# Where the key tiles of the setup are kept, and where the router's small steps stand, in a decoder layer on one core

## The chip, the core and the metric

The kernel runs on one core of one Trainium2 chip. The metric is the device time of one execution in microseconds (us); the time of a kernel is the median of its runs. The engines are named as in the profile: PE is TensorE with its matrix products (PEld its weight loads), DVE is VectorE, ACT is ScalarE, POOL is GpSimd, and SP is the engine whose queue issues the DMA transfers. A product's result lies in PSUM, in one of eight banks that the program cycles through, and is copied from there to SBUF by DVE or ACT.

## The reference, cut to what matters

One decoder layer over x of 16 x 512 x 256 (float32), in three stages, each added to x and normalised:

```
x = LN(x + self_attention(x))        # linear attention, 16 heads, two key and value maps
x = LN(x + cross_attention(x, ctx))  # 16 heads of 64; context 16 x 64 x 256
x = LN(x + experts(x))               # 8 experts, 256 -> 1024 -> 256, chosen by a router

q = x @ Wq.T
k, v = split(context @ Wkv.T)        # keys and values of the context, 1024 wide each
sim = q @ k.T / 8;  out = softmax(sim) @ v @ Wout.T + b_out
routing_weights = softmax(x @ router_w.T + router_b)
```

The change touches the setup of cross attention (the keys k of all 16 batches, and v times Wout) and the setup of the router.

## The kernel before, in words

**Stages.** Before the first batch can run, a setup of some 80 to 190 us makes what all batches share. The context (1024 rows of 256) and Wkv (2048 x 256) are loaded and transposed on PE (line 233). Then `context_rows(r, q)` makes one tile of 128 features by 512 context rows: two products of 128 x 512 (line 436), copied from PSUM to an SBUF tile named `st`. For r = 0 to 7 these are keys: there are 8 x 2 = 16 such key tiles, and each is stored to DRAM (`k_dram`, line 464). For r = 8 to 15 they are values: each tile is multiplied with Wout (`ps_vo`, line 486), the products are copied to tiles named `vst`, and these are stored to DRAM (`vo_dram`, line 491).

**Tiles.** Both `st` and `vst` are tiles of the pool `sp`. The tag `st` has two places of 512 columns, the tag `vst` four places of 2 x 264 = 528. A new tile gets the place that was given out longest ago, and the instruction that writes it waits until all that read the old tile, its store included, are done.

**The copy out of PSUM.** `evac` (lines 182 to 188) gives copies to ACT and DVE in turn, so each added or moved `evac` also changes which engine gets the following ones.

**The router.** Its weight, 8 x 256, is loaded into a corner of the tile `early`. `router_columns` (line 371) centres it on DVE (lines 374 to 376), transposes it on PE (line 379) and copies the result to the last columns of `m` (line 380). `router_weights` (line 382) transposes Wq and Wo on PE (line 389), broadcasts three biases on DVE (lines 396 and 398), and multiplies Wo and the biases with the router's columns (line 403). Wq lies in `early`, Wo in `wo`; both, and wv, are loaded by `rest_of_weights` (line 354), in which DVE adds the identity to Wq and wv (line 319).

**Beside it.** In the same stretch, the Gram products of the first batches are made (`ps_g`, lines 549 and 554, from tiles `gx` of x, two places), their block is transposed (line 567), and every four batches `key_sums` follows (line 579). The first batch's self attention begins with line 623 (`ps_gk`) and 635 (`ps_s`). `output_weights` (line 509) loads Wout in two tiles `nato` and transposes them (line 522), and multiplies them with the router's columns (line 531). Then the values begin.

**What sets the order.** Six Python generators (Grams, context, self attention, cross attention, routing, experts) emit instructions piece by piece. A small model of the engines (`Model`) estimates when each instruction ends. `weave` always continues the generator that is furthest behind its plan among those that are ready. `yield` ends a piece; `yield WAIT` ends it and holds the generator back until the model says that its last piece is through; `until(...)` holds it back until a condition holds, `made(tile)` being that the tile is written by the model's clock. The order so found is then fixed for PE, DVE, ACT and POOL (`in_order`, line 1023), so each of them works strictly in that order. The DMA issues on SP are ordered by the compiler's own scheduler, and SP too works in order.

In `all_grams` the router's steps stand between the Grams:

```
if b == 1:
    router_columns(rw)      # one piece: DVE, then PE, then DVE
    yield
if b == QB - 1:
    cs.update(rest_of_weights(sp))
    yield from router_weights(sp)
```

## Time and profile before

| | |
|---|---|
| median of 3 runs | 1394.06 us (1392.28 to 1394.08) |
| the profiled execution's own time | 1391.12 us |
| its span in the profile | 1389.4 us |
| mean granted PE clock | 0.995 |
| PE busy, 0 to 10, 10 to 20, 20 to 30, 30 to 40 us | 6.44, 6.77, 7.87, 8.83 us of 10 |
| DMA share, the same stretches | 0.74, 0.97, 0.96, 0.63 |
| stores of key tiles | 16, 256 KB each, 3.5 us to landing in the median |
| stores of value products | 132 KB each, 2.4 us to landing in the median |

The busy time of PE includes products whose ends are modelled, so a busy PE may still run at a low clock: that is read from the granted clock, which is 1.00 at full speed. A row of the timeline gives the start, the duration, the engine, the line, the operation, the tile written and the tiles read, the count of records merged in the row, and in brackets how long the engine sat idle before it and what ended that. One float32 product appears as two records, so "x8" is four products. A row of the windows gives the stretch and its length, PE's busy time with the number of records, the granted clock, the DMA share and the GB/s moved.

### The profile page before, as it was taken

The page shows a single profiled execution, that of the slowest core. Times are in us where ns is not written, and L with a number is a line of the kernel's source. Part 1 is how long each engine was busy: PE and PEld are TensorE (multiplying, and loading weights), DVE is VectorE, ACT ScalarE, POOL GpSimd, SP SyncE. Part 2 cuts the span into 40 slices and gives each one's busy share as a digit, 9 for nine tenths or more (in the row PEclk, how much of TensorE's full clock was granted, in tenths as well). Part 3 has the DMA queues.
Part 4 walks back from the last instruction along what each step waited for, and adds up shares of the span by engine and source line. Part 5 has one row for each costly group of instructions (what it writes and reads, how often), then busy time and mean ns, then how long its engine had stood idle before and what let it go on. Part 6 is the DMA issues. An engine that isn't in the chain of part 4 may idle for free.

```text
span 1389.4 us, 24206 instructions
## 1 busy us (share of the span) xinstructions
PE 1363.8 (98%) x9630; PEld 1075.8 (77%) x9630; DVE 850.5 (61%) x1957; ACT 402.2 (29%) x912; POOL 203.9 (15%) x140
## 2 busy tenths in 40 slices
PE   7999999999999999999999999999999999999997
PEld 4666676877878787878878787878888787878686
DVE  2345848466583848476584848475675939484744
ACT  1134323132232314142233223142323323232322
POOL 0001112112020111112020112112020202111200
PEclk9999999999999999999999999999999999999999
DMA  8657775511516153421606053513334061505211
GB/s 261 202 121 193 201 188 169 141 32 33 154 46 157 46 141 106 123 80 47 186 18 169 31 141 106 126 62 75 112 94 124 16 187 46 147 26 126 91 55 40
DMA packets 98373, 153.57 MB, mean 111 GB/s; under 512 B 15561, under 2 KB 70097, under 8 KB 98257
## 3 DMA queue, kind: packets, MB, share of 16 engines
q1 hardware_dynamic: 98256, 151.98, 39.9%
q8 instruction: 78, 1.28, 0.4%
q14 instruction: 39, 0.31, 0.1%
HBM read 114.71 MB, written 37.22 MB: 109 GB/s over the span
## 4 chain that ended last, share of the span: by engine, by line
PE 90%; DVE 6%; DMA 2%; ACT 1%; issue 0%; SPq 0%; DVEq 0%; ACTq 0%
PE ps_x L828 17%; PE ps_sim L808 15%; PE ps_e L957 15%; PE ps_h L940 14%; PE ps_p L705 4%; PE ps_gk L623 4%; PE ps_o L681 3%; PE ps_kv L436 3%; PE ps_t L233 2%; PE ps_vo L486 2%; PE ps_kq L745 2%; PE ps_s L635 2%; PE ps_g L549 2%; PE ps_zt L694 1%; PE ps_m L664 1%; PE ps_g L554 1%
## 5 line engine op out<-in xcount | busy, mean ns | idle before, releaser
L940 PE MATMUL ps_h<-head_T,wi 128*128 128x256 f32 x1024 | 239.1, 379 | 0.0
L828 PE MATMUL ps_x<-vo,pT 32*128 32x264 f32 x4096 | 234.4, 385 | 3.7 <-DVE pT L798 3.7
L808 PE MATMUL ps_sim<-kq,x1T 128*128 128x512 f32 x512 | 235.0, 593 | 0.0
L828 PEld LDWEIGHTS ps_x<-vo,pT 32*128 32x128 f32 x4096 | 212.5, 186 | 24.5 <-issue 5.6
L940 PEld LDWEIGHTS ps_h<-head_T,wi 128*128 128x128 f32 x1024 | 193.4, 190 | 38.8 <-issue 13.0
L796 POOL TENSOR_TENSOR s<-s,sm 128x1024 f32<-128x1024 f32 x64 | 121.8, 1903 | 539.1 <-DVE sm L795 500.7
L835 DVE TENSOR_TENSOR x<-ps_x,x 128x264 f32<-128x264 f32 x64 | 23.2, 426 | 225.6 <-PE ps_x L828 225.6
L816 ACT ACTIVATE s<-s 128x512 f32<-128x512 f32 x128 | 80.7, 630 | 276.0 <-DVE s L815 276.0
L808 PEld LDWEIGHTS ps_sim<-kq,x1T 128*128 128x128 f32 x512 | 94.5, 190 | 83.2 <-issue 74.2
L814 DVE TENSOR_REDUCE mx<-ps_sim 128x8 f32<-128x512 f32 x128 | 86.1, 672 | 42.2 <-PE ps_sim L808 41.9
L815 DVE TENSOR_TENSOR s<-ps_sim,mx 128x512 f32<-128x512 f32 x128 | 88.5, 692 | 4.4
L719 POOL TENSOR_TENSOR x<-x,bout 128x1056 f32<-128x1056 f32 x16 | 38.8, 2422 | 320.9 <-ACT hT L946 172.6
L798 DVE STREAM_TRANSPOSE pT<-s 128x1024 f32<-128x1024 f32 x64 | 78.6, 1228 | 7.0 <-POOL s L796 7.0
L946 ACT ACTIVATE hT<-ps_h 128x256 f32<-128x256 f32 x128 | 47.0, 377 | 119.9 <-PE ps_h L940 119.7
L695 ACT ACTIVATE zT<-ps_zt,shift,gain 128x512 f32<-128x512 f32 x32 | 23.2, 776 | 189.7 <-PE ps_zt L694 189.7
L794 DVE TENSOR_REDUCE sm<-s 128x16 f32<-128x1024 f32 x64 | 77.1, 1204 | 0.4 <-ACT s L816 0.4
L267 ACT ACTIVATE x<-x,off,rstd 128x264 f32<-128x264 f32 (+1 forms) x112 | 58.3, 591 | 29.3 <-DVE off L265 29.3
L681 PE MATMUL ps_o<-m,xT 128*128 128x264 f32 x256 | 66.7, 387 | 0.0
L261 ACT ACTIVATE rstd<-bn_mv,eps 128x4 f32<-128x4 f32 (+1 forms) x70 | 20.7, 295 | 158.6 <-DVE bn_mv L250 155.1
L948 DVE TENSOR_SCALAR hT<-ps_h 128x256 f32<-128x256 f32 x128 | 52.1, 409 | 22.5 <-PE ps_h L940 22.3
L705 PE MATMUL ps_p<-wo,zT 128*128 128x264 f32 x256 | 63.1, 387 | 0.0
L436 PE MATMUL ps_kv<-cT,wT 128*128 128x512 f32 x128 | 61.1, 612 | 0.2 <-ACT vst L186 0.2
(172 smaller groups left out, 1892.6 us busy)
## 6 DMA issues: line engine op xcount, KB each, us to landing
vo<-vo_dram SPq DMA_DIRECT2D x512, 132.0 KB, 4.1
vo_dram<-vst SPq DMA_DIRECT2D x128, 132.0 KB, 2.4
xt<-in_x_dram SPq DMA_DIRECT2D x16, 512.0 KB, 4.0
wi<-L_ffn_experts_inter_dram SPq DMA_DIRECT2D x8, 1024.0 KB, 5.1
gx<-in_x_dram SPq DMA_DIRECT2D x15, 512.0 KB, 4.2
x_rest<-x SPq DMA_DIRECT2D x14, 512.0 KB, 3.0
out_dram<-x SPq DMA_DIRECT2D x14, 512.0 KB, 2.9
k_dram<-st SPq DMA_DIRECT2D x16, 256.0 KB, 3.5
```

Of the source, the lines that this page charges most:

```text
L436: nc.tensor.matmul(ps, wT[:, cc, r % 4 * P:(r % 4 + 1) * P], cT[:, cc, q * 512:(q + 1) * 512], start=(cc == 0), stop=(cc == NC - 1),)
L681: nc.tensor.matmul(ps[:, :CX], xT[:, cc, t * P:(t + 1) * P], m[:, cc, :], start=(cc == 0), stop=(cc == NC - 1))
L705: nc.tensor.matmul(ps[:, :CX], zT[:, cc, t * P:(t + 1) * P], wo[:, cc, :], start=(cc == 0), stop=(cc == NC - 1))
L796: nc.gpsimd.tensor_mul(s, s, sm.unsqueeze(2).to_broadcast([P, NH, J]))
L798: nc.vector.transpose(probsT[:, :, t, :], s.rearrange("p h (a j) -> p (h a) j", a=2))
L808: nc.tensor.matmul(ps, x1T[:, cc, t * P:(t + 1) * P], kq[:, cc, hf * 512:(hf + 1) * 512], start=(cc == 0), stop=(cc == NC - 1),)
L814: nc.vector.tensor_reduce(mx[:, hs], sim, AX.X, ALU.max)
L815: nc.vector.tensor_sub(s[:, hs, :], sim, mx[:, hs].unsqueeze(2).to_broadcast([P, 8, J]))
L816: nc.scalar.activation(s[:, hs, :], s[:, hs, :], AF.Exp, scale=SCALE)
L828: nc.tensor.matmul(ps[q][:, :CX], probsT[pq, blk].rearrange("p t i -> p (t i)"), vos[c][pq, i, :], start=(c == 0 and i == 0), stop=(c == 7 ...
L940: nc.tensor.matmul(ps[:, :TB], wi[:, cc, f * P:(f + 1) * P], head_T[b][:, cc, t0 * P:t0 * P + TB], start=(cc == 0), stop=(cc == NC - 1),)
L957: nc.tensor.matmul(ps[:, :C], hT[f][:, t * P:(t + 1) * P], wo_[:, f, :], start=(f == 0), stop=(f == NF - 1),)
```

## The change

Three edits, all in the setup.

1. Key tiles of rows 1, 2, 4, 5 and 7 take their place from the tag `vst` (four places) and use its first 512 columns; rows 0, 3 and 6, and all value tiles, stay with `st` (two places). The order of key tiles runs through six places in turn.
2. `router_columns` becomes a generator with a `yield WAIT` between its steps on DVE and its transposes on PE, and begins only when `early` is written by the model's clock.
3. After `rest_of_weights` the generator ends its piece, and `router_weights` begins only when `early` and `wo` are written by the model's clock.

```diff
 def router_columns(rw):
     nc.vector.tensor_reduce(rs, rw, AX.X, ALU.add)
     nc.vector.tensor_scalar(rs, rs, -1.0 / C, 1.0 / C, ALU.mult, ALU.add)
     nc.vector.tensor_scalar(rw, rw, rs[:, 0:1], None, ALU.add)
+    yield WAIT
     ps = bank("ps_rw")
...
 def context_rows(r, q):
...
-    st = sp.tile([P, 512], FP, tag="st", name="st")
+    if r % 3 and r < NP:
+
+        st = sp.tile([P, 2, CX], FP, tag="vst", name="stk", bufs=4)
+        st = st.rearrange("p a c -> p (a c)")[:, :512]
+    else:
+        st = sp.tile([P, 512], FP, tag="st", name="st")
     evac(st, ps)
...
 def all_grams():
...
         if b == 1:
-            router_columns(rw)
+            yield from until(lambda: made(early))
+            yield from router_columns(rw)
             yield
         if b == QB - 1:
             cs.update(rest_of_weights(sp))
+            yield
+            yield from until(lambda: made(early, wo))
             yield from router_weights(sp)
```

No product, copy or transfer is added or left out. The order in which the engines meet them is made anew by `weave`.

## The prediction

> **What bounds the kernel now.** I read the page first, then the timeline of the first 75 us, then the chain of waits, then the granted clock microsecond by microsecond. The page's engine row:

> ```profile
> PE 1363.8 (98%) x9630; PEld 1075.8 (77%) x9630; DVE 850.5 (61%) x1957; ACT 402.2 (29%) x912; POOL 203.9 (15%) x140
> ```

> TensorE (PE) is busy for 98% of a span of 1389.4 us and holds 90% of the chain that ends last. A change can save only where PE stands still or runs at a low clock. The change lies in the setup, so I looked for such places between 17 us (first key product) and 82 us. The timeline shows one large hole (start, duration, engine, line; in brackets the idle time before it and what ended it):

> ```profile
> 25.99 1.88 PE L436 MATMUL ps_kv<-cT,wT 128*128 128x512 f32 x4
> ...
> 27.12 0.69 DVE L188 COPY st<-ps_kv 128x512 f32<-128x512 f32 x1 [3.79 <-DMA k_dram<-st]
> ...
> 29.47 0.69 DVE L188 COPY st<-ps_kv 128x512 f32<-128x512 f32 x1 [1.65 <-DMA k_dram<-st]
> 30.07 0.40 DVE L374 TENSOR_REDUCE rs<-early 8x1 f32<-8x256 f32 x1
> ...
> 30.68 0.34 DVE L376 TENSOR_SCALAR early<-early,rs 8x256 f32<-8x256 f32 x1
> ...
> 31.17 0.35 PE L379 MATMUL ps_rw<-ident,early 8*128 8x8 f32 x2 [3.30 <-DVE early L376]
> ...
> 31.45 3.52 PE L549 MATMUL ps_g<-gx 128*128 128x257 f32 x8
> ...
> 40.12 1.90 PE L549 MATMUL ps_g<-gx 128*128 128x257 f32 x8
> ```

> Read it from the bottom up. PE waits 3.30 us for L376, a small VectorE (DVE) step of the router. L376 is not slow: L374 to L376 take 0.95 us. They stand in DVE's order behind two copies of key tiles, and these wait for a place: `st` has two, and a place is free only when the store of its last tile has landed (3.5 us in the median). So a store holds a copy, the copy holds the router's step, and that holds PE. The other 82 us have no such hole; copies wait for stores at 48 and 54 us too, but PE does not wait for them by more than 0.3 us.

> The last two rows are the same eight matmul records: 3.52 us after the hole, 1.90 us later on. The granted clock (third number) says why:

> ```profile
> 30.00:31.00 1.00, 0.00 (x0) 1.00 1.00 311
> 31.00:32.00 1.00, 0.83 (x3) 0.58 0.88 283
> 32.00:33.00 1.00, 1.00 (x4) 0.50 0.94 279
> 33.00:34.00 1.00, 1.00 (x4) 0.50 0.52 124
> 34.00:35.00 1.00, 1.00 (x4) 0.72 0.31 2
> ...
> 75.00:76.00 1.00, 1.00 (x5) 0.76 0.00 0
> 76.00:77.00 1.00, 1.00 (x3) 0.50 0.00 0
> 77.00:78.00 1.00, 1.00 (x3) 0.50 0.00 0
> 78.00:79.00 1.00, 1.00 (x2) 0.53 0.00 0
> ```

> At half clock from about 31.16 to 34.56, and again from 75.5 to 78.9. The second follows no hole, but a run of products only 8 columns wide (L531) and transposes. A third, 338.4 to 341.8 in the same view, follows 3.25 us of idle. Each lasts 3.4 us, and they end 12 and 90 such lengths apart: the clock is decided anew every 3.41 us, from what PE did in the window before.

> **The change part by part.** PE's instruction order of the two kernels differs only among its first fifty groups; the later order of PE, DVE, ACT, POOL and SP is the same. So what the setup saves can reach the end, if nothing there waits for something else.

> *Six places for key tiles.* Rows 0, 3 and 6 use the two `st` places, the other five rows the four `vst` places, which are empty until the values begin (81 us). A tile gets a place again six tiles later: 6 x 1.72 us (two products, chain of waits) = 10.3 us, against 0.37 us of issue and 2.3 to 5.1 us to landing. The waits of copies for stores (9.0 us on DVE, 7.6 us on ScalarE, ACT) go. No work is added: 16 copies and 16 stores as before.

> *The router's pause.* Two key tiles now stand between L376 and the router's transposes on PE. The sixth tile's products end at 25.99 + 1.72 = 27.71; DVE copies it from 27.9 to 28.6 and does the router's steps by 29.6. PE needs them at 27.71 + 2 x 1.72 = 31.15. The cover is 1.6 us; without it, PE waits for the remainder and no more.

> *The path.* From 27.71 the same work lies ahead up to the point where all sixteen key tiles, L389 (weight transposes) and L623 (first Gram products) are through: ten key tiles 17.2; L379 0.28; two pairs of Gram products 2 x (1.74 + 0.89) = 5.26; transposes 0.87 + 0.22; L579 1.68; L389 1.09; L623 3.46. Sum 30.06, so 57.8 us, where before shows 63.2: **5.4 us saved**. It is made of 31.17 - 27.71 = 3.46 of hole; 3.46 - 1.74 = 1.72 of half clock on the Gram product behind it; and 0.27 before L389, which waited for DVE's additions behind a late key copy and now stands behind L623.

> *The moved weight steps.* L389 to L408 come later in the order, not longer. DVE's additions to wv and wq have their data (loads issued by 28.3 us, 4.2 us to landing) and run near 50 us; the router's products (L403) move behind the transposes of `xt`, and the broadcasts they need end on DVE near 61 us, before PE's 62.7. Cost nothing, covered by PE's own products; at most the 1 us between broadcasts and product if DVE slips. Copies that change between DVE (0.69) and ACT (0.59) lie beside PE's 1.72 per tile.

> *SP's queue and DMA.* Loads of `xt`, `xwq` and of the second pair of `gx` keep their place or gain; the first `nato` load now stands behind thirteen key stores instead of nine. The thirteenth tile's copy ends near 47.5 us, so the loads go out near 48 and 51.5 and land (4.5 us) near 52.5 and 56. They are needed near 64 and 68. The cover is 11 us; DMA's share is 0 from 66 to 83 us before, so a slip of some us fits.

> *After 58 us* everything starts 5.4 us earlier with equal distances. The stretch that DMA limits (96 us to 126 us, some 210 GB/s of value stores) begins with its own first store, so it moves along.

> [...] The closed clock at 31.16 fits the idle nearly exactly: window 27.73 to 31.15, idle 27.87 to 31.17. An idle of 3.14 us at 12.33 to 15.47, split by the same grid at 14.08, closed nothing. So the 1.72 us depend on where the grid falls. [...] This is the first rival.

> **Sum.** 5.4 us off the profiled execution's own 1391.12 us (span 1389.4, 1.7 around it) give 1385.7. That execution lies 2.9 us under the median of the runs shown, 1394.06 (they spread by 1.8), so from the median: **1388.7 us**.

> **The rivals.**
> - *The half clock was chance.* Only hole and L389 go: 3.46 + 0.27 = 3.7, so 1390.3. For it: the grid above. Against it: both holes of over 3.2 us in this execution were followed by a closure. Chance 0.24.
> - *The second closure goes too.* The order near 66 to 75 us changes: the next batch's Gram product now stands between the two blocks of 8-column products. Then 1.7 more: 1387.0. Against it: those products, with transposes ahead, now follow one another for 0.93 + 0.87 + 1.69 + 0.88 + 1.69 = 6.06 us without a dense product (5.2 before). Chance 0.08.
> - *It doesn't arrive, or is not done.* The setup moves 15 MB in its first 60 us (the windows' GB/s), with DMA's share at 0.9 to 1.1 from 20 to 33 and 40 to 49 us. If stores, not places, set the pace, the six places fill as well and a later wait (a copy, `nato`, or PE's 3.25 us of waiting for DVE at 335 us) takes the gain back: 1394. Against it: DMA's share falls to 0.14 to 0.5 at 33 to 38 us, and all the loads have 8 us and more of slack. Runs that spread as those shown can also put a gain of 3.7 under the bound. Chance 0.16.
> - *Slower.* The 6.06 us run is caught at half clock, stretches to twice its length and keeps the clock closed itself. Price 6.06 more, and 1.7 for the dense product behind it; less the sure 3.7: +4.1, 1398.2. It decides from the second closed window in a row. Against it: before's closure at 75.5 followed 1.69 + 0.93 + 1.69 of such work and opened after one window. Chance 0.04.

> **How the numbers follow.** The forecast keeps 0.48. Faster, by over 0.2% (2.8 us, about what a measurement can tell from no change): 0.48 + 0.24 + 0.08 = 0.80; within 0.2%: 0.16; slower: 0.04. The range takes in the first three cases with the runs' spread: from 1387.0 less 1.3 to 1390.3 plus 1.4, 1385.7 to 1391.7. Nothing unknown reaches beyond it by a row of its own.

> **What would show it.** Right: no copy of a key tile waits for a store; PE goes from the sixth key tile through two more into L379 without a gap; the Gram product behind takes 1.9 us; `ps_wo` (L522) starts near 64.5 instead of 70.1; the first `ps_vo` near 76 instead of 81.5; and the last product of the setup stays 5 us ahead. Wrong: PE idle in front of L379, L389 or L403; clock 0.5 for two windows in a row before 80 us; or a lead of 5 us at 80 us that is gone by 200 or 340 us.

## The result, and the profile after

The changed kernel is faster. With the result came six runs of it and six of before: median 1385.16 us (1382.98 to 1389.4) against 1393.52; ratio 0.9945, 95% interval 0.9927 to 0.9962. Two later sets of the same kernel on other occasions gave 0.9974 (0.9964 to 0.9984) and 0.9964 (0.9947 to 0.9982). All 23 runs of it have a mean of 1387.2, the 71 runs of before that came with the experiments 1392.1: **4.9 us faster, with a standard error of 0.6** (5.4 were forecast). The means of the three sets are 1385.4, 1388.2 and 1387.1, and their mean clocks 0.9962, 0.9947 and 0.9955: the faster set is the one with more clock.

The page's engine row after the change looks as before; its execution took 1389.4 us with a span of 1387.6:

```profile
PE 1365.9 (98%) x9630; PEld 1077.9 (78%) x9630; DVE 850.7 (61%) x1957; ACT 402.2 (29%) x912; POOL 203.7 (15%) x140
```

The hole in the setup is gone. PE's timeline of the changed kernel:

```profile
15.12 1.70 PE L233 MATMUL ps_t<-ident,nat 128*128 128x128 f32 x8 [2.42 <-DMA nat<-in_L_xattn_Wkv_dram]
...
27.30 5.32 PE L437 MATMUL ps_kv<-cT,wT 128*128 128x512 f32 x12
32.54 0.29 PE L380 MATMUL ps_rw<-ident,early 8*128 8x8 f32 x2
32.76 2.00 PE L555 MATMUL ps_g<-gx 128*128 128x257 f32 x8
...
63.48 1.85 PE L404 MATMUL ps_rw<-m,early 128*128 128x8 f32 x16
65.18 1.07 PE L528 MATMUL ps_wo<-ident,nato 128*128 128x128 f32 x8
66.09 2.90 PE L537 MATMUL ps_wo<-m,nato 128*128 128x8 f32 x16
68.84 3.77 PE L555 MATMUL ps_g<-gx 128*128 128x257 f32 x8
```

Three key tiles run without a gap into the router's transposes (no bracket, so no idle), and the Gram product behind them takes 2.00 us where before shows 3.52. But the next Gram product, at 68.84, takes 3.77. The timeline of all engines shows the router's step that PE had waited for, and the copy ahead of it:

```profile
29.21 0.69 DVE L188 COPY stk<-ps_kv 128x512 f32<-128x512 f32 x1 [1.14 <-PE ps_kv L437]
...
30.43 0.34 DVE L376 TENSOR_SCALAR early<-early,rs 8x256 f32<-8x256 f32 x1
```

The copy waits for its product, not for a store; L376 ends at 30.8, PE asks at 32.5. The cover is 1.8 us (1.6 forecast). The windows of the changed kernel show what happened at 68.84 (granted clock: third number):

```profile
66.00:67.00 1.00, 1.00 (x11) 0.83 0.00 0
67.00:68.00 1.00, 1.00 (x7) 0.50 0.00 0
...
72.00:73.00 1.00, 1.00 (x5) 0.50 0.00 0
73.00:74.00 1.00, 1.00 (x10) 0.76 0.00 0
```

From 66.7 to 73.5, two windows in a row, PE ran at half clock, behind the run of transposes and 8-column products (called light work below; wider products that are no transposes are called dense) that the prediction had named under its slower rival. A third window at half clock, from 15.5 to 18.9 us, lies ahead of everything that was changed, behind the wait for the first tile of Wkv: the transposes at 15.12 take 1.70 us, where before took 1.09. Before's profile lost two windows in the setup, one behind the hole and one near 75 us. So this execution lost one window more, 1.7 us. With 3.7 for the hole and L389, 2.0 should be left; its lead is 1.8.

### The profile page after: what moved, and what is told of

It reads as the page before. It is cut to its first block, busy times and chain, and to the rows that moved or that the text cites. A ratio compares the mean times of both kernels' runs of the same rounds, so it can differ in the third digit from the quotient of the medians.

```text
span 1387.6 us, 24209 instructions
## 1 busy us (share of the span) xinstructions
PE 1365.9 (98%) x9630; PEld 1077.9 (78%) x9630; DVE 850.7 (61%) x1957; ACT 402.2 (29%) x912; POOL 203.7 (15%) x140
## 4 chain that ended last, share of the span: by engine, by line
PE 89%; DVE 5%; DMA 2%; SPq 1%; ACT 1%; issue 1%; ACTq 0%; DVEq 0%
PE ps_x L834 16%; PE ps_sim L814 15%; PE ps_e L963 15%; PE ps_h L946 15%; PE ps_gk L629 4%; PE ps_p L711 4%; PE ps_o L687 3%; PE ps_kv L437 3%; PE ps_t L233 2%; PE ps_kq L751 2%; PE ps_vo L492 2%; PE ps_s L641 2%; PE ps_g L555 2%; PE ps_zt L700 1%; PE ps_m L670 1%; PE ps_g L560 1%
## 5 line engine op out<-in xcount | busy, mean ns | idle before, releaser
L687 PE MATMUL ps_o<-m,xT 128*128 128x264 f32 x256 | 66.7, 387 | 0.0
L954 DVE TENSOR_SCALAR hT<-ps_h 128x256 f32<-128x256 f32 x128 | 52.2, 409 | 22.5 <-PE ps_h L946 22.3
L629 PE MATMUL ps_gk<-wk,g 128*128 128x256 f32 x256 | 61.2, 382 | 0.0
```

Of the source, the lines that this page charges most:

```text
L629: nc.tensor.matmul(ps[:, :C], blk, wk[:, j, k, :], start=(j == 0), stop=(j == NC - 1))
L687: nc.tensor.matmul(ps[:, :CX], xT[:, cc, t * P:(t + 1) * P], m[:, cc, :], start=(cc == 0), stop=(cc == NC - 1))
```

## The experiments

Eleven sets of runs were made, of nine kernels. The ratio of each compares it with the runs of before on the same chip; "total" is the distance from the mean of all 71 runs of before. "At equal clock" is the difference that is left when one line of time against a run's mean granted clock, with the same slope for all kernels, is fitted through all runs (154 in all): 1.13 us (standard error 0.05) to each 0.001. One closed window (3.41 us at half speed) takes 0.00123 off the mean clock and 1.71 us, which would be 1.39; clocks are given to 0.001 only, and a window that closes behind the last product costs no time (in the first profile of before that product ends at 1382.96 us and the clock closes at 1386.24), which may be why the fit lies lower.

| kernel | runs | mean us | ratio to before (95%) | mean clock | total us | at equal clock us |
|---|---|---|---|---|---|---|
| before, and again | 71 | 1392.1 | | 0.9950 | | |
| changed | 23 | 1387.2 | three sets, above | 0.9953 | -4.9 | -4.6 |
| places | 12 | 1388.3 | 0.9974 (0.9964 to 0.9984) | 0.9965 | -3.8 | -2.1 |
| router | 8 | 1386.7 | 0.9959 (0.9946 to 0.9973) | 0.9965 | -5.4 | -3.7 |
| fill | 12 | 1391.7 | 0.9995 (0.9983 to 1.0008) | 0.9955 | -0.5 | 0.1 |
| places_pause | 5 | 1387.0 | 0.9963 (0.9949 to 0.9977) | 0.9962 | -5.1 | -3.7 |
| spread | 13 | 1385.8 | 0.9944 (0.9930 to 0.9957), 0.9967 (0.9953 to 0.9980) | 0.9967 | -6.3 | -4.4 |
| late | 5 | 1385.2 | 0.9951 (0.9937 to 0.9964) | 0.9976 | -7.0 | -4.0 |
| late2 | 5 | 1381.9 | 0.9929 (0.9911 to 0.9948) | 0.9976 | -10.2 | -7.2 |

The standard errors at equal clock are 0.2 to 0.45.

### before_again: the kernel before, unchanged

> The kernel before, unchanged, to see the granted clock of each timed run beside its time. What is open: the changed kernel came out 7.7 us faster by the ratio where 5.4 were worked out. If the half-clock windows are the reason (theory A: each closed window costs 1.7 us, 3.41 us at half speed, and takes 0.0012 off the mean granted clock), the timed runs of before lie on one line of time against clock, 1.7 us to each 0.0012, and their mean clock is lower than the 0.995 of the first profiled execution. If the timed runs differ for another reason (theory B), the clock does not order them. Time: 1391 to 1394.5, no change.

Ratio 1.0005 (0.9994 to 1.0016). Theory A holds in the main: its 12 runs go from 1391.0 at a clock of 0.996 to 1395.0 at 0.993, and the 31 runs of before beside them from 1387.1 at 0.998 to 1395.3 at 0.993 (correlation -0.91). Its slope was too steep: 1.1 to 1.25 us to each 0.001 in these two sets, where 1.4 were expected. Its profile also shows another hole. The timeline of before_again:

```profile
31.39 0.69 DVE L188 COPY st<-ps_kv 128x512 f32<-128x512 f32 x1 [2.40 <-DMA k_dram<-st]
...
33.09 0.35 PE L379 MATMUL ps_rw<-ident,early 8*128 8x8 f32 x2 [3.92 <-DVE early L376]
33.37 3.79 PE L549 MATMUL ps_g<-gx 128*128 128x257 f32 x8
```

The same chain, store, copy, router, PE, with a later store: 3.92 us instead of 3.30. And the clock closed for two windows behind it (32 to 39 us), with none near 75.

### places: only the six places

```diff
+            if r % 3 and r < NP:
+                st = sp.tile([P, 2, CX], FP, tag="vst", name="stk", bufs=4)
+                st = st.rearrange("p a c -> p (a c)")[:, :512]
+            else:
                 st = sp.tile([P, 512], FP, tag="st", name="st")
```

> Only the six places; the router's steps stay one piece. PE's order is that of before, so the sixth key tile is copied at 27.9 instead of 29.5 and PE's wait before L379 shrinks from 3.46 to about 1.9 us. Theory A: 1.6 us of hole saved, 0.3 before L389, and the half clock behind the hole mostly gone, since 1.9 us of idle no longer fill a window: 1.9 to 3.6 us faster, about 1390.5. Theory B, the places make up the whole gain (the router's pause moves work only): 5 us or more faster.

PE's order is exactly that of before, and the hole shrank as worked out. PE's timeline of places, then its windows:

```profile
29.45 0.26 PE L379 MATMUL ps_rw<-ident,early 8*128 8x8 f32 x2 [1.74 <-DVE early L376]
```

```profile
28.00:29.00 1.00, 0.00 (x0) 1.00 1.09 342
29.00:30.00 1.00, 0.55 (x4) 1.00 0.86 220
30.00:31.00 1.00, 1.00 (x6) 0.87 1.05 229
31.00:32.00 1.00, 1.00 (x4) 0.50 0.66 193
```

1.74 us of idle (1.9 expected). Equal clock -2.1, total -3.8, just above the expected 1.9 to 3.6. One part of the expectation fell in this execution: the clock closed all the same, at 30.74, behind a window that was idle for only half its length. In the 12 timed runs the mean clock is 0.0015 above that of before, about one closed window less in each, so the other 1.7 us of the total are clock.

### router: only the router's pause and later weight steps

The `yield WAIT`, the two `until` and the `yield` of the change, with `st` as in before.

> Only the router's pause and the later weight steps; key tiles stay with two places. Two key tiles and eight transposes now stand before L379 on PE, 4.3 us against the 3.46 of the hole, so the hole is covered though the copies still wait for stores. Theory A: 3.7 to 5.4 us faster, 1387 to 1390, close to the changed kernel. Theory B, the waiting copies hold the PSUM banks and PE waits a little later instead (around the transposes of the next weight tile, or before L389): under 2 us faster.

Faster by 5.4 in the mean, at the upper end of theory A's range. The hole before L379 went, but the profile has theory B's mechanism too, at its small size. The timeline of router:

```profile
27.12 5.32 PE L437 MATMUL ps_kv<-cT,wT 128*128 128x512 f32 x12
32.27 1.04 PE L233 MATMUL ps_t<-ident,nat 128*128 128x128 f32 x8
33.24 0.29 PE L380 MATMUL ps_rw<-ident,early 8*128 8x8 f32 x2
33.45 2.01 PE L550 MATMUL ps_g<-gx 128*128 128x257 f32 x8
...
54.29 0.69 DVE L188 COPY st<-ps_kv 128x512 f32<-128x512 f32 x1 [4.29 <-DMA k_dram<-st]
...
60.04 0.69 DVE L188 COPY st<-ps_kv 128x512 f32<-128x512 f32 x1 [3.85 <-DMA k_dram<-st]
...
60.79 0.66 PE L233 MATMUL ps_t<-ident,nat 128*128 128x128 f32 x4 [0.98 <-DVE st L188]
```

DVE's copies now wait longer for stores (22.5 us in all from 20 to 62 us, 9.0 in before), and the last of them holds the bank that the next transposes need: PE waits 0.98 us. The six places take this wait away, and at equal clock the changed kernel is 0.9 (standard error 0.4) ahead of router (-4.6 and -3.7). In the mean of the runs it is not: 1387.2 against router's 1386.7, whose runs had more clock (0.9965). So the pause alone makes most of the gain, and what the places add to it is about a microsecond at equal clock, at two standard errors.

### fill: the hole filled with products nobody reads

```diff
             nc.vector.tensor_scalar(rw, rw, rs[:, 0:1], None, ALU.add)
+            fill = psp.pool.tile([P, 512], FP, tag="ps", name="ps_fill")
+            for i, w in enumerate((512, 512, 512, 256)):
+                nc.tensor.matmul(fill[:, :w], ...)   # wT and cT again
```

> The kernel before with four added products that nobody reads (3.0 us at full clock) in the hole before L379; nothing else in PE's order changes. The hole's length stays, its idleness goes. Theory A: the half clock behind the hole goes with it, so the Gram product behind it takes 1.9 us instead of 3.5 wherever the window falls: 0 to 1.8 us faster, 1.0 to 1.7 in the mean. Theory B, the half clock does not depend on PE's idleness or falls there by chance: no change.

The timeline of fill:

```profile
30.54 3.17 PE L381 MATMUL ps_fill<-cT,wT 128*128 128x512 f32 x8
...
34.34 0.28 PE L386 MATMUL ps_rw<-ident,early 8*128 8x8 f32 x2 [0.64 <-DVE early L378]
34.56 2.01 PE L556 MATMUL ps_g<-gx 128*128 128x257 f32 x8
```

In its profile the Gram product behind the filled hole takes 2.01 us, as theory A says, and no window closes there. In the timed runs 0.5 us (standard error 0.75) is told neither from nothing nor from the lower end of the expected 1.0 to 1.7 us. That the half clock behind the hole follows PE's idleness rests on this one profile. Its own two closed windows in the setup (14.3 to 21.1 us, behind PE's wait for its first loads) lie ahead of the added products, so they are not an effect of them.

### after_again and after_third: the changed kernel, twice more

> The changed kernel, unchanged, beside before on one chip. Theory A (what the setup saves at equal clock is the hole before L379, 3.5 to 3.9 us in the two profiles of before, and 0.3 before L389; the remainder is fewer closed windows): 3.7 to 4.5 us faster at equal mean clock, 5 to 6.5 in the mean. Theory B, the six runs shown with the result were typical: 7 to 8 us in the mean, and then something besides hole and clock is saved that the profiles do not show.

> The changed kernel once more, on the chip and in the call of the two below, since its two earlier sets of runs differ (1385.4 and 1388.2 in the mean, at mean clocks of 0.9962 and 0.9947). Theory A: 1386 to 1388.5 in the mean, 4 to 5.5 us faster than before, and again the clock of a run tells its time (1.1 to 1.4 us to each 0.001).

Means 1388.2 (11 runs, clock 0.9947) and 1387.1 (6 runs, 0.9955): 4.1 and 4.3 us faster than the runs of before beside them. For after_again that is under both theories' means (5 to 6.5 and 7 to 8), while at equal clock it is 4.4, as theory A has it; after_third came out within its range. In after_third the runs go from 1384.5 at 0.998 to 1389.9 at 0.993. The profile of after_again has no closed window between 15 and 300 us and a span of 1382.1; that of after_third has two, 67 to 74 us, as in the first profile, one at 16 us, one at 183 us, and 1387.8. The six first runs were not typical: their clock was higher.

### places_pause: the weight steps left where they were

The change without the `yield` and the `until` ahead of `router_weights`.

> The six places and the pause inside the router's columns, but the weight steps (L389 to L408) where they were in before. Theory A: the hole goes whole, L389 still waits for DVE behind late additions (0.0 to 0.3): 0 to 0.5 us slower than the changed kernel at equal clock, about 1386.5 in the mean. Theory B, the later weight steps carry a part of the gain of their own: over 1 us slower than the changed kernel.

The mean is that of the changed kernel (1387.0 against 1387.2); at equal clock it is 0.9 slower, with an error of 0.5. Its five runs do not decide whether the later weight steps carry some of it. In its profile L389 starts 0.67 us after the start of the last product ahead of it, in before 0.72, where one such product follows another by 0.43. So without the later weight steps most of the 0.27 us that the prediction put there stays.

### spread and spread_again: the light work dealt out

The Wout transposes and 8-column products are issued between the last key tiles, their loads earlier:

```diff
-            yield from output_weights()          # after the keys
+            for r, q, then in ((4, 0, "out"), (4, 1, "turn"), (5, 0, "out"), (5, 1, None),
+                               (6, 0, "out"), (6, 1, "out"), (7, 0, None), (7, 1, None)):
+                key(r, q)
...
+                elif then == "out":              # a quarter of output_weights
...
+                    next(out_w, None)
```

> The changed kernel with the transposes of Wout and the 8-column products (L531 of before) dealt out between the last key tiles, and Wout loaded earlier; the work is the same. No run of light work is longer than about 3.5 us. Theory A (light work closes the clock, 1.7 us to each closed window, in most executions): no closed window between 35 and 80 us, 1 to 3 us faster than the changed kernel, mean clock up by 0.001 or more. Theory B (the second closure is rare, or light work has nothing to do with it): no change.

> Spread once more, on the same chip as the changed kernel. Theory A: equal to the changed kernel at equal clock within 0.5 us; mean clock 0.9975 or more against 0.995 to 0.996; 2 to 3.5 us faster in the mean, 1384 to 1385. Theory B (the five earlier runs were lucky): mean clock and time like the changed kernel's.

PE's timeline of spread, around one of the two light products:

```profile
44.26 1.96 PE L437 MATMUL ps_kv<-cT,wT 128*128 128x512 f32 x4
46.06 1.85 PE L565 MATMUL ps_wo<-m,nato 128*128 128x8 f32 x16
47.76 3.68 PE L437 MATMUL ps_kv<-cT,wT 128*128 128x512 f32 x8
```

In the four profiles with this order (spread twice, late, late2) no window closes between 21 and 300 us; of the nine profiles without it, five have one or two closed between 66 and 79 us. The first five runs had a mean clock of 0.9978, the next eight 0.9960, 0.4 us faster than the changed kernel beside them, where 2 to 3.5 were expected. Together the 13 runs are 1.3 us (standard error 0.7) faster than the changed kernel, with 0.0014 more clock and no gain at equal clock. The profiles speak for theory A's cause, though four are few against five of nine; the size is about half of what was expected, and not firmly above nothing.

### late and late2: the next wait, near 335 us

`late` adds a delay of eight steps of 0.5 us before the products with the probabilities of batch 1; `late2` has it at batch 2, and one behind batch 3's normalised attention.

> As spread, and batch 1's products with the probabilities (ps_x) come some 4 us later in PE's order, behind expert products that are ready, so that PE has work while DVE finishes the transposed probabilities. Theory A: the 3.25 us of idle near 335 us and the closed window behind it (338 to 342 us, in every profile so far) go: 3 to 5 us faster than spread, about 1380. Theory B: the wait only moves, to the products that follow ps_x: no change.

> Spread, with the delay that late put on the wrong batch (the idle stayed at 3.25 us) now on batch 2's probabilities, and one of the same size on batch 3's normalised attention, so that some 8 us of ready expert products stand before ps_x near 332 us. PE's order behind it changes too, the work does not. Theory A: the 3.25 us of idle and the closed window behind it go, 4 to 5 us faster than spread, 1379 to 1381. Theory B: the later order brings idle of its own, 0 to 2 us faster.

`late` was aimed at the wrong batch. The wait is that of batch 2 and stayed, here in PE's timeline of late, then of late2:

```profile
331.93 2.58 PE L862 MATMUL ps_x<-vo,pT 32*128 32x264 f32 x20 [3.25 <-DVE pT L829]
```

```profile
326.81 7.15 PE L994 MATMUL ps_e<-wo__2016,hT 128*128 128x256 f32 x32
333.80 5.34 PE L977 MATMUL ps_h<-head_T,wi 128*128 128x256 f32 x24
339.07 6.29 PE L865 MATMUL ps_x<-vo,pT 32*128 32x264 f32 x108
```

In late2 PE has expert products until DVE is done, and neither the idle nor the closed window behind it is left. It is 2.9 us faster than spread at equal clock and 3.9 in the mean (4.8 against spread's runs beside it; expected 4 to 5), though its 1381.9 lies above the expected 1379 to 1381. It is 10.2 us faster than all runs of before (9.4 than those beside it) and 5.2 faster than the changed kernel: the best version here.

## Why the prediction was right

**The hole and its chain: right.** PE's wait for L376, 3.46 us from the end of the key products, was to go. The changed kernel has no wait there; the places alone leave 1.74 (1.9 worked out); the router's pause alone removes it whole. The path behind it came out as added up: from the sixth key tile's end (27.30 + 1.72 = 29.02) to the point where all key tiles, L389 and L623 are through (59.07) the changed kernel takes 30.05 us; the sum was 30.06. It started 1.3 us later than before's 27.71, behind the closed window at 15.5. The size of the hole was that of one execution: from the end of the key products to L379 it was 3.46 in the first profile, 4.08 in before_again, and 3.80 in fill (30.54 to 34.34, filled). With their mean, 3.8, and the 0.27 before L389, 4.05 us come out at equal clock, where 4.6 (0.2) were measured. The remaining 0.5 is not settled; three profiles are few for the mean of a hole that depends on when a store lands. PE's first product of Wkv starts anywhere from 14.3 to 15.9 us in the thirteen profiles, ahead of all that was changed, so single profiles can't settle half a microsecond either.

**The half clock: the mis-sized term.** 1.72 us were counted as saved. The term was 0.1 too high as it stood, since the Gram product behind the hole takes 34.81 - 31.45 = 3.36 us to the start of the next product, not 3.46. More than that, it was counted as if each run had it. The mean clock rose from 0.99499 to 0.99530, by 0.0003, worth 0.4 us. The first rival's point, that the closed window is a matter of the grid, was right; it had no word for the windows that close elsewhere: in two of three profiles of the changed kernel, two windows close in the run of light work near 70 us, as the slower rival had it. That rival's price was wrong: the clock opened after the second window, in which most of the Gram product ran, so 3.4 us and not 7.8 were lost. One reading of the grid was off, without harm to the argument: the first two closures of before end 13 windows apart (34.56 and 78.94 us), not 12. That the clock follows what PE did in the window before was read there from three closures; thirteen profiles, with 34 of them, agree with it (last section).

**Why the sum held.** A larger hole (+0.3), another 0.5 of unknown source and a smaller clock term (-1.3) leave 4.9 of the forecast 5.4. That the errors cancel is luck; the hole, the larger part, is not. The range, 1385.7 to 1391.7, holds the mean of all runs (1387.2); the median of the six first runs, 1385.16, lies 0.5 below it, and those runs had more clock (0.9962) than the later 17 (0.9950).

**The places: right.** In the changed kernel's waits from 20 to 60 us, DVE's copies of these tiles wait for PE:

```profile
DVE stk L188 <- PE ps_kv L437: 13.8, 6, 2.9
```

Two copies to `st` and one to `stk` stand in these waits under a DMA (one of them a store), but they begin within 0.3 us of their product's end, so it is the product they waited for.

**The moved steps, SP's queue, and what follows: right.** No idle before L389 (now L390) or L403; `nato` loads issued at 49.1 and 52.6 (48 and 51.5 forecast), landing 4.8 us later, needed at 65.2 and 72.4. `ps_wo` began at 65.2 (64.5), the first `ps_vo` at 79.1 instead of 76: the forecast kept one closed window near 75 us, and the profile has one more there and one at 15.5, 3.4 us in all. The distance from there to the end is 1308.5 us against 1307.9 before, so of the lead only 0.6 us is lost behind the setup.

## What to carry to other kernels

On a kernel that PE fills to 98%, one small step of another engine that stands behind a waiting copy is worth looking for: read which instruction PE waits for, then what stands ahead of it on its own engine. Of what a hole costs, count the hole; count the half clock behind it only as a chance: here the windows fell differently in each profile of one kernel (1.8, 3.1 and 2.2 us into a window of 3.413 us, last section), and a run of light work elsewhere closed two as well (66.7 to 73.5 us). And when sets of runs of one kernel differ, look at their granted clock before looking for a cause in the code.

## What the runs showed of the hardware

Up to the last product, the half clock came in these traces in lengths of 3.413 us, or twice that in a row (6.827 us from 66.66 us in the first profile of the changed kernel). In the first profile of before the closures at 31.15, 75.52 and 338.35 us lie 13 and 77 such lengths apart. The window ahead of a closure was not always idle throughout. In places the window from 27.33 to 30.74 was idle for 1.74 us, and the clock closed; in the first profile of before, the window from 10.67 to 14.08 was idle for 1.75 us, and the clock stayed open. Windows without any idle closed it when they held almost only transposes and 8-column products (63.24 to 66.66 us in the first profile of the changed kernel), but not always. This is PE's timeline of after_again:

```profile
60.67 1.04 PE L233 MATMUL ps_t<-ident,xt 128*128 128x128 f32 x8
61.54 1.85 PE L404 MATMUL ps_rw<-m,early 128*128 128x8 f32 x16
63.24 1.07 PE L528 MATMUL ps_wo<-ident,nato 128*128 128x128 f32 x8
64.15 1.85 PE L537 MATMUL ps_wo<-m,nato 128*128 128x8 f32 x16
65.86 1.99 PE L555 MATMUL ps_g<-gx 128*128 128x257 f32 x8
```

No window closes there, in the same order of work in which two close in the first profile of the changed kernel.

Where the grid fell differed between these executions: counted in windows of 3.413 us from the start of the span, the closures of the changed kernel's three profiles at 66.66, 330.78 and 67.02 us fall 1.8, 3.1 and 2.2 us into a window, and its runs, all in the same order, go from 1383.0 us at a mean clock of 0.998 to 1391.4 at 0.993.
